# A two-layer graph attention kernel: Q of the first masked attention as a row through DRAM, behind a quarter of the graph before; carries in other PSUM banks

## The chip, the core and the metric

The kernel runs on one core of one Trainium2 chip. The time is the device time of one execution, in microseconds (us). Five runs of the kernel before have a median of 2361.38 us (2356.87 to 2363.09).

The engines go by these names: TensorE (PE; its weight loads are PEld), VectorE (DVE), ScalarE (ACT), GpSimd (POOL) and SyncE (SP), which issues transfers. Each engine takes its instructions in the order in which the program lists them.

## What is computed

Sixteen graphs of 1024 nodes with 256 features go through two layers, each on a normalised input and added back to x. One adjacency matrix serves all graphs. Cut to what matters, the reference is:

```python
def _gat(inp, adj_mask, W, a):                      # slope 0.2
    h = inp @ W
    f1, f2 = h @ a[:F_, 0], h @ a[F_:, 0]
    e = leaky_relu(f1[:, :, None] + f2[:, None, :], ALPHA)
    if adj_mask is not None:
        e = where(adj_mask[None] > 0, e, NEG_INF)
    return elu(softmax(e, axis=2) @ h)

def _L0_gnn_ref(x, adj, ...):
    out = relu(x @ mlp1_w + mlp1_b)                 # 256 -> 512
    out = elu(_gat(relu(out), None, W_fc, a_fc)) + out
    out = relu(out @ mlp2_w + mlp2_b)               # 512 -> 256
    out = elu(_gat(relu(out), adj, W_hand, a_hand)) + out
    return relu(out)

def _L1_gnn_ref(inp, adj, W, a):                    # slope 0.01, masked by adj
    return relu(softmax(e, axis=-1) @ h)

x = x + _L0_gnn_ref(relu(layernorm(x)), adj, ...)
x = x + _L1_gnn_ref(relu(layernorm(x)), adj, ...)
```

So each graph has three attentions: a dense one (no mask, 512 features), a first masked one (layer 0) and a second masked one (layer 1).

## The kernel before

**The three attentions.** The dense one isn't done as a product, except for half of graph 0. Nodes are ranked by f2 (`rank`), their rows are scattered to DRAM in that order (`scatter`), read back (`read_sorted`), and summed up from below and from above (`sum_before`, `sum_behind`). The sums go to DRAM as a fine table; the totals of each partition are summed over partitions by two small products with triangular matrices (`carry`) and written to a coarse table. Each node counts, from the sums of signs (`sign`, on ScalarE, then `count`), how many nodes lie below its threshold, and gathers its row of the fine table, then adds its row of the coarse one (`gather`, indirect transfers of GpSimd in two halves of four). `share` and `mean` turn what was gathered into the result, `merge` transposes it (hpT) for the next product.

The masked ones are products of weights with the nodes' features. The weight of node j on node i is, up to factors that cancel, the larger of Q[i] and W[j], times the mask. `vectors` makes the columns Q, W and D (tile qwd; D scales the features in `scale`). Q is needed as a row that all 128 partitions hold (`rows`). For that, `row` either broadcasts by eight transposes on TensorE into two PSUM banks and a copy on ScalarE, or, with `sent`, reads a row from DRAM into all partitions, after `send` has transposed the column, copied it and written it there. Before the change the second attention of graphs 0 to 13 goes through DRAM, and so does f2 of the dense attention (`r2`); the first attention broadcasts on TensorE. `weight` makes 128 x 256 weights on VectorE, `product` uses them for two tiles of nodes: an attention has four such quarters q, each of eight steps j. Then `finish`, `combine` and `update` (reciprocal on VectorE, exponentials on ScalarE, two adds on GpSimd for the first attention, an update of x on VectorE).

In the profile's names, tiles that end in "a" (oa, atta, hma, rowsa, pa) belong to the first masked attention, those that end in "b" (ob, attb, hmb, rowsb, pb) to the second.

**Order.** The order of every engine is written out by hand. `at(lo, hi, steps)` puts steps at planned times, in us of an ideal TensorE; all are sorted by these, and each engine takes its instructions in that order. The planned times are only an order: an engine goes on as soon as what it waits for is there. A graph b has its base at `base_of(b)` = 142 b - 28. Planned from its base: `vectors` at +1, the row at +4, the first attention's products from +11 to +39, those of the second attention of graph b-1 from +39 to +67, the norm and projection of graph b's second attention until +78, then the dense attention's merges for graph b+1, and the first projections of graph b+2. GpSimd has its own chain of dependencies in the same order; its scatters and gathers stand in it.

**Buffers.** Tiles rotate in rings by tag. `rows` has two buffers, for the dense row r2, the row of the first attention and that of the second, in the order of the program. `att` has eight. PSUM has four banks `mm` for products, two `tr` for transposes, and one pair `bc`, used for broadcasts and for `send`. The carries use `mm`.

**What the steps touch.** Lines of the kernel before: `send_row` 239 to 246, `Masked.send` and `row` 353 to 364, `weight` 373, `product` 384, Gnn0's finish 396 to 413, Gnn1's 420 to 426, `rank` 511 to 518, `scatter` 525, `sign` 548, `read_sorted` 569, `sum_before` and `sum_behind` 597 to 612, `write_table` 604, `carry` 615 to 624, `gather` 635, `share` 647, `mean` 657 and 659, `merge` 706; in the plan `dense_sums`, `gathers`, `masked_first`, `second_norm`, `masked_second` and the loop over graphs at the end.

Of the kernel before, what the change touches and what calls it, by code (L numbers as in the profile page):

```python
# [8 lines left out]
F32 = mybir.dt.float32  # L9
# [8 lines left out]
P = 128  # L18
HALF = 512
# [12 lines left out]
def fast_path(ctx: ExitStack, tc: tile.TileContext, alarm, x, adj, w1, b1, w2, b2, w_fc, a_fc,  # L32
# [21 lines left out]
    nc = tc.nc  # L54
    NB, N, F = x.shape
    H = w1.shape[1]
    NT = N // P
# [12 lines left out]
    dram = ctx.enter_context(tc.tile_pool(name="dram", bufs=1, space=bass.MemoryType.DRAM))  # L70

    def mm_psum(name):
        return psum.tile([P, HALF], F32, tag="mm", name=name, bufs=4)
# [4 lines left out]
    def bc_psum(name):  # L78
        return psum.tile([P, NH * HALF], F32, tag="bc", name=name, bufs=1)


    def load_x(b, name):
        xt = big.tile([P, NT, F], F32, tag="x", name=f"{name}_{b}", bufs=3)
        src = x[b].rearrange("(t p) f -> p t f", p=P)
        for part in ((slice(0, TH), slice(TH, NT)) if name == "xn" and b == 0 else (slice(0, NT),)):
# [17 lines left out]
                            base=0, channel_multiplier=-1)  # L103
# [75 lines left out]
    sorted_d = [nc.dram_tensor(f"sorted{k}", [N, R], F32, kind="Internal").ap() for k in range(2)]  # L179
    fine_d = [dram.tile([N + 1, 2 * K], F32, name=f"fine{k}") for k in range(2)]  # L180
    coarse_d = [dram.tile([P + 1, 2 * K], F32, name=f"coarse{k}") for k in range(2)]
    row_d = {s: [dram.tile([1, N], F32, name=f"row_{s}{k}") for k in range(2)] for s in "rb"}
    zero = work.tile([1, K], F32, tag="carry", name="zero", bufs=2)
    nc.vector.memset(zero, 0.0)
    for k in range(2):
# [33 lines left out]
    NQ = N // PAIR  # L219
    ATT = 8  # L220

    def at(lo, hi, steps):
        for i, step in enumerate(steps):
            table.append((lo + (hi - lo) * i / len(steps), len(table), step))
# [15 lines left out]
    def send_row(dst, col, name):  # L240

        ps = bc_psum(f"{name}_ps")
        nc.tensor.transpose(ps[:NT, :P], col, ident)
        line = work.tile([NT, P], F32, tag="carry", name=name, bufs=2)
        nc.scalar.copy(line, ps[:NT, :P])
        nc.sync.dma_start(dst.rearrange("o (u i) -> (o u) i", i=P), line)

    class Norm:

# [52 lines left out]
    class Masked:  # L302
# [2 lines left out]

        def __init__(self, get_hT, w_sb, slope, b, which):
            self.get_hT, self.w_sb, self.slope, self.name = get_hT, w_sb, slope, f"{which}_{b}"
            self.b = b
            self.hm = None
            self.att = {}  # L310
            self.out = {}
# [39 lines left out]
            nc.vector.tensor_scalar_max(qwd[:, 2, :], qwd[:, 2, :], D_MIN)  # L351

        def send(self):
            send_row(row_d["b"][self.b % 2], self.qwd[:, 0, :], f"line{self.name}")

        def row(self, sent=False):

            self.rows = work.tile([P, N], F32, tag="rows", name=f"rows{self.name}")
            if sent:
                nc.sync.dma_start(self.rows, row_d["b"][self.b % 2].to_broadcast([P, N]))  # L360
            else:
                rows_ps = bc_psum(f"rowsps{self.name}")
                row_broadcast(rows_ps, cols(self.qwd[:, 0, :]))
                nc.scalar.copy(self.rows, rows_ps)  # L364
# [67 lines left out]
    class Dense:  # L432
# [182 lines left out]
        def carry(self, s):  # L615
            lhsT, total = ((upto, self.all_t), (after, self.xs[0][:, 0, :]))[s]
            carry = work.tile([P, K], F32, tag="carry", name=f"carry_{self.b}_{s}", bufs=2)
            for lo, n in ((0, F + 1), (F + 1, F)):
                ps = mm_psum(f"carry_{self.b}_{s}_{lo}")
                nc.tensor.matmul(ps[:, :n], lhsT=lhsT, rhs=total[:, lo:lo + n], start=True,  # L620
                                 stop=True)
                nc.scalar.copy(carry[:, lo:lo + n], ps[:, :n])
            coarse = coarse_d[self.b % 2]
            nc.sync.dma_start(coarse[:P, K:] if s else coarse[1:P + 1, :K], carry)

# [122 lines left out]
    xs = {}  # L748
# [17 lines left out]
    def each(f, *ranges):  # L766
        out = [()]
        for r in ranges:
            out = [o + (i,) for o in out for i in r]
        return [partial(f, *o) for o in out]  # L770
# [41 lines left out]
    def dense_sums(t0, b):  # L812
        d = dense[b]
        at(t0 - 3, t0 - 3, [d.sums_begin])
        at(t0 - 22, t0 - 4, each(d.sign, range(NT)))
        for h in range(2):
            at(t0 + 6.5 + 4 * h, t0 + 6.5 + 4 * h, [partial(d.sums_weights, h)])
            at(t0 + 7.5 + 5 * h, t0 + 12.5 + 5 * h, each(d.sum_before, tiles(h)))
        at(t0 + 13, t0 + 13, [partial(d.write_table, 0, 0)])
        at(t0 + 18, t0 + 18, [partial(d.write_table, 0, 1)])  # L820
        at(t0 + 18, t0 + 32, each(d.sum_behind, range(NT - 1, -1, -1)))
        at(t0 + 25, t0 + 25, [partial(d.write_table, 1, 1)])
        at(t0 + 32, t0 + 32, [partial(d.write_table, 1, 0)])
        at(t0 + 33, t0 + 33, [d.count])
        at(t0 + 50.5, t0 + 50.5, each(d.carry, range(2)))

    def gathers(d, h, lo, hi):
        at(lo, lo + 4, each(d.gather, [h], [0], range(TH)))
        at(hi, hi + 7, each(d.gather, [h], [1], range(TH)))
# [25 lines left out]
    def weights(m, q, lo, hi):  # L855
        at(lo, hi, each(m.weight, [q], range(NT)))

    def masked_first(t0, b):
        m, n = gnn0[b], norm2[b]
        at(t0 + 1, t0 + 1, [m.vectors])  # L860
        at(t0 + 4, t0 + 4, [m.row])
        at(t0 + 4.5, t0 + 10, each(m.scale, range(NT)))
        weights(m, 0, t0 + 5.5, t0 + 10)
        at(t0 + 10, t0 + 10, [partial(load_again, b)])
        at(t0 + 4.5, t0 + 11, each(dense[b].natural, range(NT // 2)))
        at(t0 + 11, t0 + 39, each(m.product, range(NQ), range(NT)))
        for q in range(1, NQ):
            weights(m, q, t0 + 5.5 + 7 * q, t0 + 12 + 7 * q)
        for t in range(NT):
            lo = t0 + 18.2 + 7 * (t // 2) + 0.6 * (t % 2)  # L870
            at(lo, lo, [partial(m.finish, t)])
            at(lo + 1.2, lo + 1.2, [lambda t=t: m.combine(t, dense[b].o_nat)])
            at(lo + 5.2, lo + 5.2, [lambda t=t: m.update(t, xs[b])])
            at(lo + (6.2 if last(b) or b == 0 else 9), lo + (6.2 if last(b) or b == 0 else 9), [partial(n.stats, t)])
        at(t0 + 36, t0 + 36, [partial(n.root, 0)])
        lo = t0 + (46.5 if last(b) or b == 0 else 51)
        at(lo, lo, [partial(n.root, 1)])

    def last(b, n=1):
        return b >= NB - n  # L880

    def second_norm(t0, b):
        n, m = norm2[b], gnn1[b]
        if last(b):
            n.turn_at(t0 + 46.5, 0)
            n.turn_at(t0 + 49, 1, 1.6)
            lo = t0 + 50
        elif b == 0:
            n.turn_at(t0 + 47, 0)
            n.turn_at(t0 + 50.5, 1, 1.6)  # L890
            lo = t0 + 47.2
        else:
            n.turn_at(t0 + 53.3, 0)
            n.turn_at(t0 + 67.3, 1)
            lo = t0 + 71
        at(lo, lo + 7, each(m.project, range(NT)))
        at(lo + 7.5, lo + 7.5, [m.extremes])
        if last(b, 2):
            at(lo + 7.8, lo + 7.8, [m.vectors])
            at(lo + 8.2, lo + 8.2, [m.row])  # L900
            at(lo + 8.3, lo + 9.5, each(m.scale, range(NT)))
        else:
            at(lo + 11, lo + 11, [m.vectors])
            at(lo + 24, lo + 24, [m.send])
            at(lo + 40, lo + 52, each(m.scale, range(NT)))
            at(base_of(b + 1) + 22, base_of(b + 1) + 22, [partial(m.row, True)])

    def masked_second(parts, b):

# [14 lines left out]


    SHORT = 28.0

    def base_of(b):
        return b * PERIOD - SHORT * (b > 0)

# [9 lines left out]
    n = norm1[1]  # L940
# [59 lines left out]
    for b in range(NB):  # L1000
        base, after_base = base_of(b), base_of(b + 1)
        masked_first(base, b)
        second_norm(base, b)
        if last(b):
            parts = [base + 65 + 7 * q for q in range(NQ)]
        elif last(b, 2):
            parts = [base + 86, base + 94.5, base + 107.5, after_base + 39]
        else:
            parts = [after_base + 39 + 7 * q for q in range(NQ)]
        masked_second(parts, b)  # L1010
        if b + 1 < NB:
            if b:
                dense_sums(base, b + 1)
            for h in range(NH):
                if b:
                    gathers(dense[b + 1], h, base + 48 + 4 * h, base + 58 + 7 * h)
                else:
                    gathers(dense[1], h, base + 16 + 12 * h, base + 22 + 25 * h)
            dense_end(after_base - PERIOD, b + 1)
        if b + 2 < NB:  # L1020
            first_mlp(base, b + 2)
            dense_rows(after_base - PERIOD, b + 2)
            dense_begin(after_base, b + 2)
        if b + 3 < NB:
            lo = after_base - PERIOD + 86
            at(lo, lo, [partial(load_first, b + 3)])
            first_norm(after_base, b + 3)
# [465 lines left out]
```

## Time and profile before

| | |
|---|---|
| median of 5 runs | 2361.38 us |
| the profiled execution | 2360.6 us, of which 2358.9 span |
| granted TensorE clock, mean | 0.991 |
| TensorE, VectorE, ScalarE, GpSimd busy | 97%, 70%, 53%, 41% |
| products of the two masked attentions (line 384) | 455.8 + 459.7 us busy |
| a steady graph (start of one oa product to the next) | 139.9 us |

The profile is of one execution. Times in it count from the span's start. A line of the order in time has start, duration, engine, line, operation, out<-in, shape and count; in brackets the idle time before and what ended it. Neighbouring instructions of one kind are merged into one such line, and as TensorE's instructions overlap, what a group costs is read from its start to the start of the next. Each product of 32-bit floats shows as two passes, a transpose as one. The graph followed below is 5: its base lies near 859.4 us, its first oa product starts at 870.17.

### The profile page before, as it was taken

How to read it: one execution, taken by the hardware profiler on the slowest of the kernel's cores; microseconds unless marked ns; L12 is line 12 of the kernel's file. 1: busy time of each engine (PE TensorE's matmuls, PEld its weight loads, DVE VectorE, ACT ScalarE, POOL GpSimd, SP SyncE). 2: the span in 40 equal slices, each digit the busy share in tenths (PEclk: the TensorE clock that was granted, in tenths of full speed). 3: DMA queues.
4: the chain of work that ended last, by engine and by line, in shares of the span. 5: the costliest groups of instructions: out<-in, count | busy, mean ns of one | idle time of the engine just before them, and what ended most of it. 6: DMA issues, size and time to landing. Idle time of an engine off the chain costs nothing.

```text
span 2358.9 us, 31110 instructions
## 1 busy us (share of the span) xinstructions
PE 2281.7 (97%) x10053; PEld 1759.3 (75%) x10053; DVE 1639.4 (70%) x4499; ACT 1250.1 (53%) x2740; POOL 968.3 (41%) x1216
## 2 busy tenths in 40 slices
PE   8989999999999999999999999999999999999897
PEld 5666777777877777777787877777787777778666
DVE  6766685866958577685866868586686857759554
ACT  5345655646365563745646374564736556463442
POOL 1153444353534536344353634435353453535220
PEclk9999999999999999999999999999999999999898
DMA  4658256572645746265573635657264574726400
GB/s 170 169 152 214 65 156 185 154 199 89 195 107 170 188 137 188 86 182 152 168 190 116 185 98 162 176 161 197 88 199 102 167 188 142 191 80 203 109 1 29
DMA packets 148522, 348.41 MB, mean 148 GB/s; under 512 B 10776, under 2 KB 62200, under 8 KB 144256
## 3 DMA queue, kind: packets, MB, share of 16 engines
q1 hardware_dynamic: 102400, 182.36, 26.3%
q0 software_dynamic: 45952, 163.99, 25.9%
q8 instruction: 82, 1.34, 0.2%
q14 instruction: 88, 0.72, 0.1%
HBM read 220.06 MB, written 126.24 MB: 147 GB/s over the span
## 4 chain that ended last, share of the span: by engine, by line
PE 60%; DVE 30%; ACT 5%; issue 2%; POOL 2%; DMA 1%; DVEq 0%; ACTq 0%; POOLq 0%; SPq 0%
PE ob L384 12%; PE h L465 11%; PE oa L384 9%; PE m L451 8%; PE m L724 5%; DVE attb L373 5%; PE pb L322 5%; DVE atta L373 4%; DVE junk L513 4%; DVE junk L511 3%; DVE xs L612 3%; DVE x L413 2%; PE hpT L706 2%; PE pa L322 2%; DVE stats L262 2%; PE nt L282 2%
## 5 line engine op out<-in xcount | busy, mean ns | idle before, releaser
L384 PE MATMUL oa<-hma,atta 128*128 128x258 f32 x2048 | 455.8, 382 | 12.1 <-DVE atta L373 12.1
L465 PE MATMUL h<-wfc_sb,resT 128*128 128x257 f32 x2048 | 466.0, 380 | 0.0
L384 PE MATMUL ob<-hmb,attb 128*128 128x257 f32 x2048 | 459.7, 384 | 5.5 <-DVE attb L373 5.5
L384 PEld LDWEIGHTS oa<-hma,atta 128*128 128x128 f32 x2048 | 384.5, 190 | 78.5 <-DVE atta L373 23.5
L384 PEld LDWEIGHTS ob<-hmb,attb 128*128 128x128 f32 x2048 | 392.1, 192 | 62.0 <-ACT hmb L368 3.7
L465 PEld LDWEIGHTS h<-wfc_sb,resT 128*128 128x128 f32 x2048 | 378.9, 190 | 53.5 <-issue 1.0
L717 POOL TENSOR_TENSOR resT<-resT,e 128x512 f32<-128x512 f32 x128 | 163.3, 1276 | 416.6 <-DVE e L716 371.9
L373 DVE SCALAR_TENSOR_TENSOR atta<-rowsa,qwda,edge 128x256 f32<-128x256 f32 x512 | 263.6, 542 | 43.8 <-ACT rowsa L364 31.2
L373 DVE SCALAR_TENSOR_TENSOR attb<-rowsb,qwdb,edge 128x256 f32<-128x256 f32 x512 | 257.0, 531 | 30.8 <-PE ob L384 28.0
L408 POOL TENSOR_TENSOR posa<-posa,onat 128x256 f32<-128x256 f32 x120 | 106.8, 890 | 408.7 <-ACT posa L400 408.7
L451 PE MATMUL m<-hT,w_sb 128*128 128x512 f32 x512 | 236.9, 601 | 0.5 <-ACT posa L400 0.5
L399 ACT ACTIVATE ea<-oa,reca 128x256 f32<-128x256 f32 x128 | 60.8, 475 | 329.0 <-DVE reca L396 318.5
L724 PE MATMUL m<-resT,w_sb 128*128 128x512 f32 x512 | 230.8, 597 | 4.4 <-POOL resT L717 4.4
L635 POOL DMA_INDIRECT got<-coarse,k x124 | 194.6, 1570 | 39.8 <-issue 39.8
L422 ACT ACTIVATE rb<-ob,recb 128x256 f32<-128x256 f32 x128 | 57.5, 474 | 269.7 <-DVE recb L420 269.7
L708 DVE TENSOR_SCALAR e<-hpT 128x512 f32<-128x512 f32 x128 | 88.4, 691 | 150.3 <-PE hpT L706 112.4
L724 PEld LDWEIGHTS m<-resT,w_sb 128*128 128x128 f32 x512 | 94.1, 192 | 107.3 <-issue 91.6
L451 PEld LDWEIGHTS m<-hT,w_sb 128*128 128x128 f32 x512 | 92.8, 193 | 91.5 <-issue 88.8
L635 POOL DMA_INDIRECT got<-fine,k x124 | 129.6, 1045 | 61.7 <-issue 29.1
L548 ACT ACTIVATE junk<-r,fs 128x1024 int8<-128x1024 f32 x124 | 142.7, 1151 | 12.3 <-POOL fs L469 12.1
L525 POOL DMA_INDIRECT sorted<-hnat,place x128 | 131.5, 1028 | 39.5 <-issue 16.4
L709 ACT ACTIVATE e<-e 128x512 f32<-128x512 f32 x128 | 80.7, 630 | 93.3 <-DVE e L708 93.0
(183 smaller groups left out, 3495.8 us busy)
## 6 DMA issues: line engine op xcount, KB each, us to landing
xs<-sorted SPq DMA_DIRECT2D x32, 1028.0 KB
fine<-tt SPq DMA_DIRECT2D x32, 1026.0 KB
fine<-xs SPq DMA_DIRECT2D x32, 1026.0 KB
x<-in_x_dram SPq DMA_DIRECT2D x16, 1024.0 KB
out_dram<-x SPq DMA_DIRECT2D x32, 512.0 KB
xn<-in_x_dram SPq DMA_DIRECT2D x15, 1024.0 KB
coarse<-carry SPq DMA_DIRECT2D x32, 256.5 KB
r<-row_r SPq DMA_DIRECT2D x14, 512.0 KB
```

The costliest lines, as they stand in the source:

```text
L322: nc.tensor.matmul(ps[:, :2 + F], lhsT=hT[:, c, t * P:(t + 1) * P], rhs=self.w_sb[:, c, 0, :], start=(c == 0), stop=(c == FC - 1))
L373: nc.vector.scalar_tensor_tensor(a_t, self.rows[:, q * PAIR:(q + 1) * PAIR], self.qwd[:, 1, j:j + 1], edge[:, j, q * PAIR:(q + 1) * PAIR], ...
L384: nc.tensor.matmul(self.out[t][:, :F + self.ONES], lhsT=self.att[q, j][:, (t % 2) * P:(t % 2 + 1) * P], rhs=self.hm[:, j, 2:2 + F + self.O ...
L408: adder.tensor_add(pos, pos, o_nat[:, t, :])
L451: nc.tensor.matmul(ps, lhsT=w1_sb[:, kc, c * P:(c + 1) * P], rhs=hT[:, kc, h * HALF:(h + 1) * HALF], start=(kc == 0), stop=(kc == FC - 1))
L465: nc.tensor.matmul(ps[:, :F + 1], lhsT=self.resT[:, kc, t * P:(t + 1) * P], rhs=wfc_sb[:, kc, g, :], start=(kc == 0), stop=(kc == HC - 1))
L513: nc.vector.tensor_scalar(junk[:, t * P:], r2[:, t * P:], s, None, op0=OP.is_lt, op1=OP.add, accum_out=rank[:, 1, t:t + 1])
L525: made = nc.gpsimd.indirect_dma_start(out=sorted_d[self.b % 2], out_offset=bass.IndirectOffsetOnAxis(ap=self.place[:, t:t + 1], axis=0), i ...
L548: nc.scalar.activation(junk, self.r2, AF.Sign, bias=self.fs[:, 0, t:t + 1], accum_out=self.signs[:, t:t + 1])
L635: nc.gpsimd.indirect_dma_start(out=got[u // n][:, u % n, :], out_offset=None, in_=(coarse_d if coarse else fine_d)[self.b % 2][:, :], in_o ...
L717: nc.gpsimd.tensor_add(dst, dst, e)
L724: nc.tensor.matmul(ps, lhsT=w2_sb[:, kc, c * P:(c + 1) * P], rhs=self.resT[:, kc, h * HALF:(h + 1) * HALF], start=(kc == 0), stop=(kc == H ...
```

## The change

It has five parts.

1. The first attention of graphs 1 to 14 (`AHEAD`) sends Q through DRAM: `send` planned at +3.4 and the read at +6, in place of the broadcast at +4. Its products start at +18 instead of +11; its weights, finishes, statistics and roots move with them.
2. The first quarter of graph b-1's second attention (b-1 from 0 to 13) goes from +39 to +11, the other three stay at +46, +53 and +60 or move there. Its row is read at -4.5 instead of +22.
3. `carry` uses the pair `bc` instead of two `mm` banks for each; the two carries stand at +38.9 and +45.9 instead of both at +50.5. The gathers are planned 3 to 4 us sooner.
4. `send_row` issues its write from ScalarE instead of SP.
5. The signs are spread by hand from -27 to -8.2 (before: from -22, 2.25 apart, the last at -6.25). The first half of norm2 is turned at +60.3 instead of +53.3.

```diff
-    row_d = {s: [...] for s in "rb"}
+    row_d = {s: [...] for s in "rab"}
...
     def send_row(dst, col, name):
...
         nc.scalar.copy(line, ps[:NT, :P])
-        nc.sync.dma_start(dst.rearrange("o (u i) -> (o u) i", i=P), line)
+        nc.scalar.dma_start(dst.rearrange("o (u i) -> (o u) i", i=P), line)
...
         def carry(self, s):
...
-            for lo, n in ((0, F + 1), (F + 1, F)):
-                ps = mm_psum(f"carry_{self.b}_{s}_{lo}")
-                nc.tensor.matmul(ps[:, :n], lhsT=lhsT, rhs=total[:, lo:lo + n], start=True,
-                                 stop=True)
-                nc.scalar.copy(carry[:, lo:lo + n], ps[:, :n])
+            ps = bc_psum(f"carry_{self.b}_{s}")
+            parts = ((0, F + 1, 0), (F + 1, F, HALF))
+            for lo, n, bank in parts:
+                nc.tensor.matmul(ps[:, bank:bank + n], lhsT=lhsT, rhs=total[:, lo:lo + n],
+                                 start=True, stop=True)
+            for lo, n, bank in parts:
+                nc.scalar.copy(carry[:, lo:lo + n], ps[:, bank:bank + n])
...
     def dense_sums(t0, b):
-        at(t0 - 22, t0 - 4, each(d.sign, range(NT)))
+        for t, lo in enumerate((27, 25, 18.5, 16.3, 14.1, 12, 9.8, 8.2)):
+            at(t0 - lo, t0 - lo, [partial(d.sign, t)])
...
-        at(t0 + 50.5, t0 + 50.5, each(d.carry, range(2)))
+        at(t0 + 38.9, t0 + 38.9, [partial(d.carry, 0)])
+        at(t0 + 45.9, t0 + 45.9, [partial(d.carry, 1)])
...
     def masked_first(t0, b):
         at(t0 + 1, t0 + 1, [m.vectors])
-        at(t0 + 4, t0 + 4, [m.row])
-        at(t0 + 4.5, t0 + 10, each(m.scale, range(NT)))
-        weights(m, 0, t0 + 5.5, t0 + 10)
+        lo = t0 + 11
+        if b in AHEAD:
+            at(t0 + 3.4, t0 + 3.4, [m.send])
+            at(t0 + 6, t0 + 6, [partial(m.row, True)])
+            lo += 7
+        else:
+            at(t0 + 4, t0 + 4, [m.row])
+        at(t0 + 4.5, lo - 1, each(m.scale, range(NT)))
+        weights(m, 0, lo - 5.5, lo - 1)
...
-        at(t0 + 11, t0 + 39, each(m.product, range(NQ), range(NT)))
+        at(lo, lo + 28, each(m.product, range(NQ), range(NT)))
...
-        at(t0 + 36, t0 + 36, [partial(n.root, 0)])
-        lo = t0 + (46.5 if last(b) or b == 0 else 51)
+        at(lo + 25, lo + 25, [partial(n.root, 0)])
+        lo += 35.5 if last(b) or b == 0 else 38.5
         at(lo, lo, [partial(n.root, 1)])
...
     def second_norm(t0, b):
-            n.turn_at(t0 + 53.3, 0)
+            n.turn_at(t0 + 60.3, 0, 7)
             n.turn_at(t0 + 67.3, 1)
...
-            at(base_of(b + 1) + 22, base_of(b + 1) + 22, [partial(m.row, True)])
+            at(base_of(b + 1) - 4.5, base_of(b + 1) - 4.5, [partial(m.row, True)])
...
+    AHEAD = range(1, NB - 1)
...
-            parts = [after_base + 39 + 7 * q for q in range(NQ)]
+            parts = [after_base + lo for lo in (11, 46, 53, 60)]
...
-                    gathers(dense[b + 1], h, base + 48 + 4 * h, base + 58 + 7 * h)
+                    gathers(dense[b + 1], h, base + 44.5 + 3.5 * h, base + 55 + 7 * h)
```

More of the change, by code (lines that the diff above doesn't have):

```diff
@@ L181, in fast_path @@
     coarse_d = [dram.tile([P + 1, 2 * K], F32, name=f"coarse{k}") for k in range(2)]
-    row_d = {s: [dram.tile([1, N], F32, name=f"row_{s}{k}") for k in range(2)] for s in "rb"}
+    row_d = {s: [dram.tile([1, N], F32, name=f"row_{s}{k}") for k in range(2)] for s in "rab"}
     zero = work.tile([1, K], F32, tag="carry", name="zero", bufs=2)
@@ L307, in __init__ @@
             self.get_hT, self.w_sb, self.slope, self.name = get_hT, w_sb, slope, f"{which}_{b}"
-            self.b = b
+            self.b, self.which = b, which
             self.hm = None
@@ L353, in send @@
         def send(self):
-            send_row(row_d["b"][self.b % 2], self.qwd[:, 0, :], f"line{self.name}")
+            send_row(row_d[self.which][self.b % 2], self.qwd[:, 0, :], f"line{self.name}")
         def row(self, sent=False):
@@ L359, in row @@
             if sent:
-                nc.sync.dma_start(self.rows, row_d["b"][self.b % 2].to_broadcast([P, N]))
+                nc.sync.dma_start(self.rows, row_d[self.which][self.b % 2].to_broadcast([P, N]))
             else:
@@ L860, in masked_first @@
         at(t0 + 1, t0 + 1, [m.vectors])
-        at(t0 + 4, t0 + 4, [m.row])
-        at(t0 + 4.5, t0 + 10, each(m.scale, range(NT)))
-        weights(m, 0, t0 + 5.5, t0 + 10)
+        lo = t0 + 11
[7 more added lines that the diff above has]
+        weights(m, 0, lo - 5.5, lo - 1)
         at(t0 + 10, t0 + 10, [partial(load_again, b)])
         at(t0 + 4.5, t0 + 11, each(dense[b].natural, range(NT // 2)))
-        at(t0 + 11, t0 + 39, each(m.product, range(NQ), range(NT)))
+        at(lo, lo + 28, each(m.product, range(NQ), range(NT)))
         for q in range(1, NQ):
-            weights(m, q, t0 + 5.5 + 7 * q, t0 + 12 + 7 * q)
+            weights(m, q, lo - 5.5 + 7 * q, lo + 1 + 7 * q)
         for t in range(NT):
[L870 to L874, printed above, removed]
-        at(t0 + 36, t0 + 36, [partial(n.root, 0)])
-        lo = t0 + (46.5 if last(b) or b == 0 else 51)
+            end = lo + 7.2 + 7 * (t // 2) + 0.6 * (t % 2)
+            at(end, end, [partial(m.finish, t)])
+            at(end + 1.2, end + 1.2, [lambda t=t: m.combine(t, dense[b].o_nat)])
+            at(end + 5.2, end + 5.2, [lambda t=t: m.update(t, xs[b])])
+            end += 6.2 if last(b) or b == 0 else 9
+            at(end, end, [partial(n.stats, t)])
+        at(lo + 25, lo + 25, [partial(n.root, 0)])
+        lo += 35.5 if last(b) or b == 0 else 38.5
         at(lo, lo, [partial(n.root, 1)])
```

## The prediction

> **What bounds the kernel now.** I read the page's head first, then TensorE's waits over the whole run, then one steady period by stages, then the orders in time of TensorE, VectorE and GpSimd in it. The head says that TensorE is busy 97% of the span. In a steady period of 140 us it is busier still:
>
> ```profile
> PE 2281.7 (97%) x10053; PEld 1759.3 (75%) x10053; DVE 1639.4 (70%) x4499; ACT 1250.1 (53%) x2740; POOL 968.3 (41%) x1216
> ...
> 857.00:997.00 140.00, 138.76 (x615) 106.98 (x614) 99.22 (x272) 77.02 (x171) 62.50 (x78) 1.00 0.55 155
> ...
> PE oa L384 <- DVE atta L373: 12.1, 28, 0.8
> PE hpT L706 <- DVE hp L659: 6.4, 7, 1.7
> ...
> PE pa L322 <- ACT hma L324: 3.5, 14, 0.6
> ```
>
> The second line is the stretch from 857 to 997 us: its length, then busy time of TensorE, weight load, VectorE, ScalarE and GpSimd, the granted clock (1.00), the DMA share and GB/s. Only 1.2 us of 140 are idle. So a steady graph gets shorter in two ways: less TensorE work, or less of that 1.2 us; and any new wait is paid in full. The last lines are waits over the whole run (total, times, longest). The 28 waits for the weights of the first masked attention (oa) are two in each of graphs 1 to 14.
>
> Why these come is in VectorE's load by stage (same columns):
>
> ```profile
> 865.90:870.40 4.50, 4.40 (x24) 2.78 (x23) 1.67 (x4) 3.81 (x9) 0.00 (x0) 1.00 0.97 397
> 870.40:911.80 41.40, 40.47 (x185) 34.35 (x183) 40.92 (x94) 17.05 (x44) 16.74 (x20) 1.00 0.53 141
> 911.80:931.40 19.60, 19.57 (x96) 16.67 (x97) 13.12 (x40) 4.92 (x12) 15.98 (x14) 1.00 0.94 299
> ```
>
> From 870.4 to 911.8 VectorE has 40.92 of 41.40 us to do: the sums of the next graph's table, the weights, the updates. It falls behind and TensorE meets it in the last quarter. In the 4.5 us before, it waits for the sorted rows; in the 20 us after, the DMA engines are the full resource (0.94), with the gathers.
>
> **What TensorE loses of work.** Now eight broadcast transposes of Q run in each graph:
>
> ```profile
> 863.80 1.04 PE L238 MATMUL rowspsa<-ident,qwda 128*128 128x128 f32 x8
> 864.67 1.88 PE L451 MATMUL m<-hT,w_sb 128*128 128x512 f32 x4
> ...
> 911.78 1.13 PE L620 MATMUL carry<-all,upto 128*128 128x257 f32 x4
> 912.95 1.14 PE L620 MATMUL carry<-xs,after 128*128 128x257 f32 x4
> 913.92 2.76 PE L384 MATMUL ob<-hmb,attb 128*128 128x257 f32 x12
> ```
>
> They hold TensorE from 863.80 to 864.67, 0.87 us, 0.109 each (their 273 ns overlap). One transpose (send) stays, so 7 x 0.109 = 0.76 us go in each of 14 graphs (AHEAD is 1 to 14): 10.7 us. ScalarE loses the 1.01 us copy of the broadcast and gets a copy of 0.24 us (the row of line<-line_ps).
>
> The carries: from 911.78 to 913.92 they take 2.14 us for eight passes; at the rate of the products beside them (12.30 us for 56 passes, 0.220 each) they need 1.76. The other 0.38 us are waits for the evictions of the shared "mm" banks. In two free banks, 7 us apart, they go: 14 x 0.38 = 5.3 us. In graphs 0 and 1 the two carries still stand together, now with one pair of banks: the second waits for two copies, 0.81 us and a hand-over of 0.2, so +1.0 each, +2.0.
>
> **What the moved quarter does for VectorE.** Counted with the spacing of its rows (weights 0.40, sums 0.67, pairs of reciprocals 0.14, updates 0.34, statistics 0.54), VectorE has 24.3 us to do up to the last oa weights, plus 3 us of slowing beside GpSimd's adds (pairs of weights take 1.8 instead of 0.87): 27.3, from 870.4 to 897.7, where TensorE wanted them at 897.3. Afterwards 4.6 us more come ahead of them (five weights of the moved quarter, the first three fall into the gap before; its updates; four oa weights that now run in that gap; the count), and the sums begin 0.7 us sooner, with TensorE, so they end near 901.6; TensorE, with the 7 us of the moved quarter and one carry ahead, wants them at 904.4. The 12.1 us of waits go. Bounds: all 12.1, or none if VectorE slips 3 us more; I take all, the margin being 2.8 us.
>
> **The new way of Q.** The transpose is at 863.8, the copy ends near 864.4, then write and read in series. The same pair for the dense rows: write issued 832.65, read issued 833.88 (1.2 us); the 512 KB then move for some 4 us. That gives 870.0, and 872.5 when it shares the engines with the 2 MB of sorted rows (share 0.97). SP has the read behind that of the sorted rows (which waits for the scatters until 863.66) and ahead of x for the update, which goes from 864.9 to 866: needed only 20 us later. VectorE gets to the first oa weight at 874.1, as the sums and the moved quarter's weights stand before it. So the cover is 1.6 us, and 2.3 us more before TensorE needs that weight at 876.4: cost nothing; with the cover gone, each us late is a us of TensorE in 14 graphs. The row of the second attention now leaves right behind the dense row, 25 us before its use. The Trainium skill (DMA: Bandwidth & Descriptors, Anatomy of one DMA — SWDGE (gpsimd) path) puts some 2 us of fixed cost on every DMA, mostly completion, which speaks against two in series; this trace has 1.2 us for the small one; by the page Q would be 0.8 us later, still covered.
>
> An issue on ScalarE is not in this trace. Bounds: nothing, and 0.41 us (two issues of SP take 0.82); three in a graph, with ScalarE at 55%, each behind the copy it sends. I take nothing for TensorE; queued behind are evictions that have four banks.
>
> **Signs and scatters.** Two signs move to the time before the projections and the other six go up to 2 us earlier in ScalarE's order; the last now stands before the first eviction of pa, which frees the bank for TensorE's fifth pa tile. Today that sign starts at 855.11, after GpSimd has copied its column at 854.88, behind five scatters 1.5 to 1.95 us apart. With two signs (2.7 us) out of the way, the eviction that lets GpSimd begin is some 0.8 us earlier, the last sign ends near 855.5, the eviction at 855.95, and TensorE wants the bank at 855.4: 0.5 us of wait instead of 0.25 (3.5 us in all now). Bounds: -0.25 and +1.0 a graph. I take +0.25: +3.5.
>
> **Where the wait can go: the gathers.** The chain that is closest behind TensorE in a steady graph:
>
> ```profile
> 910.21 1.08 POOL L635 DMA_INDIRECT got<-fine,k  x1 [0.17 <-issue]
> ...
> 929.03 1.54 POOL L635 DMA_INDIRECT got<-coarse,k  x1 [0.30 <-issue]
> ...
> 941.18 0.16 DVE L647 TENSOR_TENSOR den<-got,qd 128x4 f32<-128x4 f32 x1 [7.73 <-DMA got<-coarse,k]
> ...
> 943.56 2.29 DVE L659 SCALAR_TENSOR_TENSOR hp<-got,den,part 128x513 f32<-128x513 f32 x3
> ...
> 945.57 0.67 PE L706 MATMUL hpT<-ident,hp 128*128 128x128 f32 x4
> ```
>
> Half 0's last coarse gather is issued at 929.03, lands at 941.2, and the last hp is there at 945.85; the fourth transpose starts at 945.90. TensorE doesn't wait, by 0.05 us. In the period before (hp until 805.11, transpose at 806.06) the slack is 0.95; over the thirteen steady graphs 0.7 on average. TensorE will be here 0.76 + 0.38 + 0.85 = 2.0 us sooner. Does the chain come sooner? The adds of the last oa quarter, which gate all gathers today, will end near 917.5, but three fine gathers go ahead of them, from about 909. Then adds, fine ones, the first coarse one, the norm's root (1.5 us) and three coarse ones follow, the last issued near 930 to 931, 1 to 2 us later than now. Landing is by the DMA engines, though (12 us after issue), and the carries' 0.51 MB (at 299 GB/s, 1.7 us) no longer lie among the gathers. Landing between 1.7 us sooner and 1.9 later; I take 0.6 sooner, on the side of the DMA's rows. The wait is 2.0 - 0.7 - 0.6 = 0.7 us, for graphs 2 to 14: 13 x 0.7 = 9.1. Bounds: no wait (2.0 - 0.7 - 1.7 is below nothing), and 2.0 - 0.7 + 1.9 = 3.2, or 41.6. The same root feeds the second half of norm2 (nt): its result is due near 927 and TensorE comes at 928.
>
> **Sum.** The profiled execution took 2360.6 us (span 2358.9 and 1.7 around it). 2360.6 - 10.7 - 5.3 - 12.1 + 2.0 + 3.5 + 9.1 = 2347.1. The median of the runs shown is 0.8 above that execution: 2348.
>
> **Rivals.** (1) *All of it comes*: the gathers keep pace with TensorE and the signs cost nothing: 2360.6 - 28.1 + 2.0 = 2334.5, 2335 for the median. For it: DMA freed of the carries; against: a slack of 0.05 to 0.95 us where 2 are taken away. (2) *Given back at hpT*: a wait of 1.9 us, 24.7: 2338.0 + 24.7 = 2362.7, no change. It takes landing 0.6 us later than now. (3) *Slower, by GpSimd's order*: the root and the adds stand among the gathers, the DMA engines can't make it up, half 0 lands 1.9 us later, and hpT waits 3.2: 2338.0 + 41.6 = 2379.6. It decides from a wait of about 2.2 us. For it: GpSimd's stream is without a gap from 909 on; against: the 12 us from issue to landing. (4) *Q isn't hidden*: the row lands 4.5 us later than I think, at 877.0, the first oa weight is there at 877.5, and TensorE waits 1.1 us: 14 x 1.1 = 15.4, 2363; the end of TensorE's waits is then only swapped for another.
>
> **Chances.** Forecast (2340 to 2356) 0.46; (1) 0.22; (2) 0.10 and (4) 0.04, both no change; (3) 0.18. What can be told from no change is about 0.2%: under 2356.7 is faster, 0.68; within 0.14; above 2366.1 slower, 0.18. The range reaches from just under rival (1) to rival (2): 2332 to 2364.
>
> **What will show it.** Right: rowspsa in two graphs only; no oa waits for atta in steady graphs; carry rows of 0.9 us; a steady period near 138.9 us. Wrong, and where: waits at hpT for hp over 2 us a graph (gathers); at pa for hma over 0.6 (signs); at nt for hn (root); at oa's first quarter for atta (Q's row late); or the first ob quarter waiting for attb.

## The result, and the profile after

The kernel after takes 2364.75 us (median of 28 runs, 2359.49 to 2373.41), the kernel before 2360.43 (50 runs, 2354.83 to 2364.08). The ratio is 1.0023, with a 95% interval of 1.0016 to 1.003: slower by 0.2%. The forecast of a gain of 0.5% was wrong, in sign too, and the time lies just above its range. The profiled execution of after took 2363.13 us (span 2361.4, clock 0.993).

First the page's head, then TensorE's waits over the whole run (total, times, longest):

```profile
PE 2262.2 (96%) x9955; PEld 1746.6 (74%) x9955; DVE 1611.6 (68%) x4499; ACT 1242.8 (53%) x2740; POOL 954.0 (40%) x1216
```

```profile
PE extpsb L238 <- DVE extb L330: 25.0, 14, 3.6
...
PE ob L384 <- DVE attb L373: 14.1, 21, 2.1
PE hpT L708 <- DVE hp L661: 6.9, 8, 1.7
PE oa L384 <- DVE atta L373: 5.2, 12, 1.6
...
PE pa L322 <- ACT hma L324: 0.8, 2, 0.4
```

The work did go: TensorE is busy for 19.5 us less (2281.7 before). But the span is 2.5 us longer, so 22.0 us of new idle time have come. The list says where: 25.0 us at extpsb and 14.1 at ob; oa gives back only 6.9 of its 12.1. In the kernel before these two rows were:

```profile
PE ob L384 <- DVE attb L373: 5.5, 3, 2.1
...
PE extpsb L238 <- DVE extb L330: 1.5, 2, 0.8
```

The stretch from 866.55 to 1006.4 is a steady period of after, from one transpose extpsa to the next. Over graphs 2 to 13 such a period takes 140.3 us on average, where before took 139.6 and the prediction had 138.9. By stages (length, busy time of TensorE, weight load, VectorE, ScalarE, GpSimd, then granted clock, DMA share, GB/s):

```profile
871.00:912.00 41.00, 40.63 (x189) 34.39 (x188) 36.59 (x83) 18.76 (x48) 9.28 (x11) 1.00 0.68 190
912.00:932.00 20.00, 18.68 (x89) 15.60 (x88) 14.01 (x44) 4.76 (x12) 17.09 (x19) 1.00 0.69 221
932.00:950.00 18.00, 17.39 (x70) 12.10 (x69) 6.33 (x20) 9.68 (x21) 10.70 (x8) 1.00 1.07 232
```

VectorE's full stage is relieved, as meant: 36.59 of 41 us, where it had 40.92 of 41.40. TensorE's idle time now lies in the two later stages, 1.32 and 0.61 us in this period.

**The wait at extpsb.** VectorE's order in time, then TensorE's:

```profile
945.80 0.17 DVE L649 TENSOR_TENSOR den<-got,qd 128x4 f32<-128x4 f32 x1 [8.36 <-DMA got<-coarse,k]
...
948.11 0.16 DVE L330 TENSOR_REDUCE extb<-hmb 128x1 f32<-128x8 f32 x1
```

```profile
948.34 0.29 PE L238 MATMUL extpsb<-ident,extb 128*128 128x128 f32 x1 [0.61 <-DVE extb L330]
```

The tile extb holds the extremes of the second attention's values hmb, and has nothing to do with the gathers. It stands behind `share` in VectorE's order, and `share` waits 8.36 us for the gathered rows. So TensorE waits for the landing of half 0 (the moment its gathered rows are there and `share` can start), through an instruction that has only its place in the queue from it. This was the meeting that the prediction priced at hpT; it comes some 2 us earlier, at extpsb.

In graphs 2 to 13, against the start of the same graph's extpsa, the fourth coarse gather has been issued (its GpSimd instruction has ended) at 68.1 us before and 70.6 after (means), and `share` starts at 78.4 before and 79.8 after. So issue is 2.5 us later, landing 1.4 us later, while TensorE comes sooner.

**The wait at ob.** GpSimd's order in time while this happens, and VectorE's:

```profile
914.61 1.11 POOL L637 DMA_INDIRECT got<-fine,k  x1 [0.20 <-issue]
916.03 0.96 POOL L637 DMA_INDIRECT got<-fine,k  x1 [0.30 <-issue]
917.30 0.94 POOL L637 DMA_INDIRECT got<-fine,k  x1 [0.30 <-ACT ea L405]
918.25 0.74 POOL L408 TENSOR_TENSOR posa<-posa,onat 128x256 f32<-128x256 f32 x1
919.07 0.72 POOL L409 TENSOR_TENSOR ea<-ea,posa 128x256 f32<-128x256 f32 x1
...
930.16 1.14 POOL L268 TENSOR_TENSOR rstd<-rstd,power 128x4 f32<-128x4 f32 x1
...
935.40 1.55 POOL L637 DMA_INDIRECT got<-coarse,k  x1 [0.30 <-issue]
```

```profile
919.83 0.42 DVE L413 SCALAR_TENSOR_TENSOR x<-ea,x 128x256 f32<-128x256 f32 x1 [2.03 <-POOL ea L409]
920.17 0.48 DVE L373 SCALAR_TENSOR_TENSOR attb<-rowsb,qwdb,edge 128x256 f32<-128x256 f32 x1
923.91 0.43 DVE L413 SCALAR_TENSOR_TENSOR x<-ea,x 128x256 f32<-128x256 f32 x1 [3.27 <-POOL ea L409]
924.26 0.48 DVE L373 SCALAR_TENSOR_TENSOR attb<-rowsb,qwdb,edge 128x256 f32<-128x256 f32 x1
```

The adds of tiles 6 and 7 now stand between the gathers. VectorE's updates wait for them (2.03 and 3.27 us), and behind each update is a weight for ob that needs nothing from it. Over the run VectorE's waits (total, times, longest) say the same; before, the first line had 93.5 and the second 3.0:

```profile
DVE den L649 <- DMA got<-coarse,k: 136.9, 25, 11.4
...
DVE x L413 <- POOL ea L409: 64.7, 29, 3.3
...
DVE atta L373 <- DMA rowsa<-row_a: 11.8, 12, 3.3
```

The last line is Q on its way. Orders of issue of the queues, and VectorE's first oa weight (in the same period):

```profile
869.43 0.27 ACTq L246 DMA_DIRECT2D row_a<-linea  x1
...
874.83 0.32 SPq L360 DMA_DIRECT2D rowsa<-row_a  x1
...
879.55 0.48 DVE L373 SCALAR_TENSOR_TENSOR atta<-rowsa,qwda,edge 128x256 f32<-128x256 f32 x1 [1.13 <-DMA rowsa<-row_a]
```

The read follows the write by 5.4 us, not by the 1.2 us that the pair of the dense row needed.

### The profile page after: what moved, and what is told of

Read it like the earlier page. It is cut to its first block, busy times and chain, and to the rows that moved or that the text cites. A ratio compares the mean times of both kernels' runs of the same rounds, so it can differ in the third digit from the quotient of the medians.

```text
span 2361.4 us, 30815 instructions
## 1 busy us (share of the span) xinstructions
PE 2262.2 (96%) x9955; PEld 1746.6 (74%) x9955; DVE 1611.6 (68%) x4499; ACT 1242.8 (53%) x2740; POOL 954.0 (40%) x1216
## 5 line engine op out<-in xcount | busy, mean ns | idle before, releaser
L384 PE MATMUL ob<-hmb,attb 128*128 128x257 f32 x2048 | 463.0, 383 | 14.2 <-DVE attb L373 14.1
L384 PEld LDWEIGHTS ob<-hmb,attb 128*128 128x128 f32 x2048 | 385.8, 191 | 78.7 <-ACT rb L422 12.6
L408 POOL TENSOR_TENSOR posa<-posa,onat 128x256 f32<-128x256 f32 x120 | 100.8, 840 | 471.6 <-ACT posa L400 471.1
L373 DVE SCALAR_TENSOR_TENSOR attb<-rowsb,qwdb,edge 128x256 f32<-128x256 f32 x512 | 237.0, 505 | 9.9 <-PE ob L384 7.3
L451 PE MATMUL m<-hT,w_sb 128*128 128x512 f32 x512 | 237.8, 603 | 0.5 <-ACT posa L400 0.5
L726 PEld LDWEIGHTS m<-resT,w_sb 128*128 128x128 f32 x512 | 93.5, 191 | 106.1 <-issue 90.4
L451 PEld LDWEIGHTS m<-hT,w_sb 128*128 128x128 f32 x512 | 93.5, 194 | 93.1 <-issue 90.7
```

The source lines that it names most:

```text
L373: nc.vector.scalar_tensor_tensor(a_t, self.rows[:, q * PAIR:(q + 1) * PAIR], self.qwd[:, 1, j:j + 1], edge[:, j, q * PAIR:(q + 1) * PAIR], ...
L384: nc.tensor.matmul(self.out[t][:, :F + self.ONES], lhsT=self.att[q, j][:, (t % 2) * P:(t % 2 + 1) * P], rhs=self.hm[:, j, 2:2 + F + self.O ...
L408: adder.tensor_add(pos, pos, o_nat[:, t, :])
L451: nc.tensor.matmul(ps, lhsT=w1_sb[:, kc, c * P:(c + 1) * P], rhs=hT[:, kc, h * HALF:(h + 1) * HALF], start=(kc == 0), stop=(kc == FC - 1))
L726: nc.tensor.matmul(ps, lhsT=w2_sb[:, kc, c * P:(c + 1) * P], rhs=self.resT[:, kc, h * HALF:(h + 1) * HALF], start=(kc == 0), stop=(kc == H ...
```

## The experiments

Each is compared with the kernel before on its own chip; times are medians.

**Is the landing of half 0 what costs?** *less_after* leaves out two of its four coarse gathers in graphs 1 to 15, and the mean of tiles 2 and 3 takes the rows of tiles 0 and 1. *less_before* does the same to the kernel before. *ext_first* keeps all gathers and puts the extremes (extb) ahead of `share`.

```diff
         def gather(self, h, coarse, u):
+            if coarse and h == 0 and u >= 2 and not self.split:
+                return
...
-        at(lo + 7.5, lo + 7.5, [m.extremes])
+        at(lo + 6.9, lo + 6.9, [m.extremes])
```

> The changed kernel without two of the four coarse gathers of half 0 in graphs 1 to 15 (mean then uses the rows of tiles 0 and 1 for tiles 2 and 3, so those tiles' dense attention is left wrong). Theory G (the gathered rows of half 0 land too late for TensorE, and that eats the gain): landing comes some 5 us sooner, the 25.0 us of waits of extpsb for extb vanish, and the time falls from 2364.8 to some 2340. Rival O (VectorE's other lateness, Q's late row and updates behind GpSimd's adds, is what costs): waits move elsewhere and the time stays above 2355.

> The kernel before, with the same two gathers left out (tiles 2 and 3 of half 0 get the rows of tiles 0 and 1). Theory G: TensorE did not wait for the gathers there, so nothing: 2360 within 3 us. If the gathers bounded the kernel before too, it falls by more than 10 us.

> The changed kernel with extremes of the second attention ahead of share in VectorE's order, so that extps waits for the gathers no longer. Theory G: the wait only moves 1.7 us on, from extpsb to hpT, and the time stays within 4 us of 2364.8. Rival (only VectorE's order costs, hpT itself has room): the 25 us go, and the time falls to 2340 to 2345.

*less_after*: 2335.16 us, 0.9882 (0.9867 to 0.9897). *less_before*: 2357.78, 0.9989 (0.998 to 0.9998). *ext_first*: 2363.79, 1.0015 (1.0006 to 1.0025). Two gathers less bring some 30 us where TensorE has been made faster, and 3 where it hasn't: a gain of the expected size is there, and half 0 keeps it back. It isn't the expected sum term by term: in the profiled execution of *less_after* the wait at extpsb is the 1.5 us of before, while ob still waits 16.6 us. The edit also takes bytes from the DMA engines, so it doesn't yet say why half 0 is late. With the extremes ahead of `share` the wait at extpsb is again the 1.5 us of before, but hpT, where TensorE needs the gathered rows themselves, has taken it over: 12.8 us more of waits (6.9 us in 8 waits in after), and hpT's rows busy for 84.5 us instead of 77.8:

```profile
PE hpT L708 <- DVE hp L661: 19.7, 39, 1.7
```

So the order of extb and `share` is only where the lateness shows.

**What makes half 0 late: GpSimd's order or the DMA engines?** *dve_adds* puts the adds of tiles 6 and 7 of the first attention, in graphs 1 to 14, on VectorE. *adds_first* leaves them on GpSimd and puts all gathers behind them, as they stood before. *dve_adds_before* is the first edit on the kernel before.

```diff
-            adder = nc.vector if self.beside_gathers else nc.gpsimd
+            adder = nc.vector if self.beside_gathers or (self.b in AHEAD and t >= 6) else nc.gpsimd
...
-                    gathers(dense[b + 1], h, base + 44.5 + 3.5 * h, base + 55 + 7 * h)
+                    gathers(dense[b + 1], h, base + 48.1 + 3.5 * h, base + 55.2 + 7 * h)
```

> The changed kernel with the two adds of tiles 6 and 7 of the first attention on VectorE instead of GpSimd, in graphs 1 to 14. Theory P (GpSimd's stream, with those adds and the root among the gathers, makes half 0 late): four adds of 0.73 us go out of the stream, the last coarse gather of half 0 is issued some 3 us sooner, it lands 2 to 3 us sooner, extpsb's 25 us of waits go to under 5, and the updates no longer wait for GpSimd, so ob's waits fall from 14 to 6: some 2335 to 2340. Theory D (the DMA engines are full, so issue does not matter): landing stays, only ob's waits go: some 2356.

> The changed kernel with the gathers planned from +48.1, behind all adds of the first attention. Theory P: GpSimd idles some 1 us for the adds' operands and the stream ends that much later; extpsb waits 35 to 40 us in all, ob's waits fall by 8: 2366 to 2372. If the updates behind the adds were what costs, not the landing: some 2356.

> The kernel before with the same two adds on VectorE. TensorE waits there for VectorE's weights and not for the gathers, and VectorE has no room until 911.8: no gain, 2360 to 2366. If the gathers bound the kernel before as well, it gets faster.

*dve_adds*: 2329.12 us, 0.9879 (0.9858 to 0.99), faster than both kernels and some 6 us below the expected 2335. GpSimd's stretch of the same gathers, in this run:

```profile
901.10 1.08 POOL L637 DMA_INDIRECT got<-fine,k  x1 [0.20 <-issue]
902.48 0.96 POOL L637 DMA_INDIRECT got<-fine,k  x1 [0.30 <-issue]
903.75 1.18 POOL L637 DMA_INDIRECT got<-fine,k  x1 [0.30 <-issue]
905.23 0.96 POOL L637 DMA_INDIRECT got<-fine,k  x1 [0.30 <-issue]
...
914.04 1.07 POOL L268 TENSOR_TENSOR rstd<-rstd,power 128x4 f32<-128x4 f32 x1
...
919.14 1.55 POOL L637 DMA_INDIRECT got<-coarse,k  x1 [0.30 <-issue]
```

From the first fine gather to the start of the fourth coarse one it is 18.0 us, against 20.8 in after (914.61 to 935.40); over graphs 2 to 13 the means are 18.1 and 20.8, and 18.2 in before. The first fine gather starts at the same place in all three, 47.7 to 48.3 us behind extpsa, so the later issue of after is these adds. Issue is 3.3 us sooner on average (67.3 against 70.6), `share` 3.7 us sooner (76.0 against 79.8). The DMA engines move the same bytes, so it was not they that kept half 0 late. The weights for ob no longer stand behind an add on another engine. TensorE's waits (extpsb is back at the 1.5 us of before; ob is not, 9.6 where 6 were expected):

```profile
PE ob L384 <- DVE attb L373: 9.6, 16, 2.1
...
PE oa L384 <- DVE atta L373: 1.8, 6, 0.4
...
PE extpsb L238 <- DVE extb L330: 1.5, 2, 0.8
```

*adds_first*: 2411.55 us, 1.0225 (1.0209 to 1.024): the sign was right and the size far off. The waits:

```profile
PE nt L282 <- DVE hn L272: 36.9, 22, 9.8
PE extpsb L238 <- DVE extb L330: 36.7, 15, 3.4
```

The wait at ob is the old 5.5 us, so the adds among the gathers did cause that one. Half 0 comes later still (`share` at 81.3), and now the root is late as well (nt waits 21.2 us more than in after). In the profiled executions (2403.36 and 2363.13 us) these waits and the ones that shrink make 20.8 us; the other 20.1 are TensorE's busy time, 2282.3 instead of 2262.2 for the same instructions. Of it 13.6 lie in the products m behind extpsb (251.4 instead of 237.8) and 5.6 in nt, at a mean granted clock of 0.981 instead of 0.993; the last section has the reason.

*dve_adds_before*: 2396.52 us, 1.0163 (1.0148 to 1.0179), where no gain was expected and a loss of 36 us came. VectorE's order at the tiles 6 and 7:

```profile
915.09 0.42 DVE L408 TENSOR_TENSOR posa<-posa,onat 128x256 f32<-128x256 f32 x1 [0.90 <-ACT posa L400]
916.66 0.43 DVE L409 TENSOR_TENSOR ea<-ea,posa 128x256 f32<-128x256 f32 x1 [1.15 <-ACT ea L406]
917.00 0.51 DVE L373 SCALAR_TENSOR_TENSOR attb<-rowsb,qwdb,edge 128x256 f32<-128x256 f32 x1
```

Directly behind the last oa quarter VectorE has no lead: it waits for ScalarE's eviction and exponential, 2.05 us in this graph, with the weights for ob behind, and ob's waits go from 5.5 to 33.1 us. The same edit gains 1.5% of the kernel after (2364.75 to 2329.12) and costs 1.6% of the kernel before.

**Does Q's row cost?** *sp_send* takes part 4 back: the row is written from SP's queue.

```diff
-        nc.scalar.dma_start(dst.rearrange("o (u i) -> (o u) i", i=P), line)
+        nc.sync.dma_start(dst.rearrange("o (u i) -> (o u) i", i=P), line)
```

> The changed kernel with the three row writes issued from SP again. Now the read of Q's row is issued 5.4 us after its write, where the quiet write took 1.2, as 2 MB of sorted rows are under way. If that is the shared DMA engines, the queue makes no difference or SP's is worse (its write stands behind the sorted rows in one queue): 2364.8 to 2370. If the second queue itself costs: faster by 5 or more.

2390.28 us, 1.0129 (1.0105 to 1.0153), some 26 us more than after and 20 above what was expected. SP's issues and TensorE's wait:

```profile
875.98 0.28 SPq L246 DMA_DIRECT2D row_a<-linea  x1
883.20 0.32 SPq L360 DMA_DIRECT2D rowsa<-row_a  x1
```

```profile
PE oa L384 <- DVE atta L373: 17.7, 28, 2.2
```

Behind the sorted rows in SP's queue the 4 KB take 7.2 us, and oa waits 12.5 us more than in after. TensorE's busy time grows by another 17.1 (2279.3), again for the same instructions and at a lower granted clock (0.988). The prediction had taken part 4 as free; it was worth these 26 us.

**The smaller parts, alone.** *carry_alone* and *sign_alone* are the kernel before with part 3 without the move of the gathers, and with the signs of part 5.

```diff
-        at(t0 + 50.5, t0 + 50.5, each(d.carry, range(2)))
+        at(t0 + 38.9, t0 + 38.9, [partial(d.carry, 0)])
+        at(t0 + 45.9, t0 + 45.9, [partial(d.carry, 1)])
...
-        at(t0 - 22, t0 - 4, each(d.sign, range(NT)))
+        for t, lo in enumerate((27, 25, 18.5, 16.3, 14.1, 12, 9.8, 8.2)):
+            at(t0 - lo, t0 - lo, [partial(d.sign, t)])
```

> The kernel before with the carries alone changed: in the bc banks, at +38.9 and +45.9, gathers where they were. By the prediction's sum 14 x 0.38 = 5.3 us less and 2.0 more in graphs 0 and 1: some 2357. Theory G adds that 0.38 us a graph fits in the slack of 0.7 at hpT, so it should come; if it does not, the slack is smaller than read.

> The kernel before with the signs' order alone changed. The prediction had pa's waits for hma grow by 3.5 us; in the changed kernel they fell from 3.5 to 0.8. If the order of the signs did that, they fall here too, and the time by 2 to 3 us, 2357.5, near what can be told; if not, pa's waits stay at 3.5 or grow to 7.

*carry_alone*: 2361.88 us, 1.0004 (0.9995 to 1.0013): nothing, where 3 to 4 us were expected. The carries' products did get shorter, 38.7 us instead of 41.4 in the run, but the next meeting took it, the turn of norm2, where the kernel before has 15.8 us in 8 waits:

```profile
PE nt L282 <- DVE hn L272: 18.5, 17, 9.9
```

*sign_alone*: 2356.8 us, 0.998 (0.997 to 0.9989), a gain of 3.6 us, and the waits at pa for hma fall from 3.5 us to 0.9.

**Do they matter beside the adds?** *dve_carry_back* is dve_adds with `carry` and its time as before the change; *dve_adds_ext* is dve_adds with the extremes ahead of `share`.

> dve_adds with the carries back in the mm banks, both at +50.5. If the prediction's 0.38 us a graph is real and only hidden where something later in the graph is the bound (carry_alone gave nothing, as the turn of norm2 then waited), it must show here, where TensorE has no long wait: 14 x 0.38 = 5.3 us, less 2.0 at the start: 2329.1 + 3.3, some 2332; more if the 0.5 MB among the gathers makes half 0 late again. If the carries' banks never mattered: 2329 within 2.

> dve_adds with extremes ahead of share. Half 0 now lands some 3 us before TensorE comes, so no wait is left to move: 2329 within 3 us. If the order behind share still cost, it gets faster by more than 4.

*dve_carry_back*: 2363.99 us, 1.0011 (0.9998 to 1.0024), about 32 more than expected. TensorE's waits, and GpSimd's:

```profile
PE carry L620 <- ACT carry L622: 18.3, 15, 1.3
...
PE carry L620 <- ACT posa L400: 7.8, 14, 0.6
```

```profile
POOL got L635 <- DMA coarse<-carry: 30.7, 14, 3.0
```

At the old time the banks "mm" still hold the last oa quarter, which the change has moved there, and the coarse table comes 2 to 3 us late for the first coarse gather. A part that alone is worth nothing is worth some 30 us in the new order.

*dve_adds_ext*: 2334.6 us, 0.989 (0.9876 to 0.9905), no gain over dve_adds (0.9858 to 0.99). That is 5.5 us above dve_adds and outside the expected 3, but the two ran on different chips and their intervals overlap.

## Why the prediction was wrong

The sum by its own terms, for the profiled executions; measured values are differences of the rows and waits of the two traces:

| term | predicted us | measured us |
|---|---|---|
| seven transposes of Q | -10.7 | -10.8 (rowspsa 16.7 to 2.1, linea_ps 3.8 new) |
| carries | -5.3 + 2.0 | -3.1 (products -2.7, pauses 2.3 to 1.9) |
| oa waits for atta | -12.1 | -6.9 |
| pa waits for hma | +3.5 | -2.7 |
| half 0 of the gathers | +9.1 | +24.0 (extpsb +23.5, hpT +0.5) |
| ob waits for attb | 0 | +8.6 |
| not in the sum | 0 | -6.6 |
| span | -13.5 | +2.5 |

The last line but one is what is left; 6.0 of it is busy time of TensorE outside the rows and carries. The carries are part of it: read from start to start, as the prediction did, they take 1.74 us instead of 2.14 in each of graphs 2 to 15, 5.6 us, and 1.1 more in graphs 0 and 1, together -4.5 instead of -3.1. The transposes on and nt are the largest other groups (busy for 2.9 and 2.6 us less); why stays open. The execution of the table has the highest clock of after's 30 (0.993; the median is 0.9885), so it is not the typical one.

**Right:** the work that TensorE loses (10.8 us of transposes for 10.7, 0.40 us a graph of carries for 0.38), and that the closest chain behind it, GpSimd's gathers, decides. Rival (1), "all of it comes", at 2335, is near what *less_after* measured when the chain was lightened, 2335.16; that it is the same number is luck, as ob waited there and *dve_adds* went below it. GpSimd's issue was right too: "the last issued near 930 to 931" is 930.82 in after, once the 4.58 us are taken off by which this graph's extpsa starts later.

**The step that failed:** "Landing is by the DMA engines, though … I take 0.6 sooner, on the side of the DMA's rows." The 12 us from issue to landing were read as a queue in full DMA engines that would swallow a later issue. With issue 2.5 us later, landing is 1.4 later: the engines made up 1.1, where the step let them make up 1.6 to 2.6 (issue 1 to 2 later, landing 0.6 sooner). *dve_adds* settles it: the same bytes, issued 3.3 us sooner, are there 3.7 us sooner. The wait is then 2.0 us on average in twelve steady graphs (0.6 to 3.6), in place of 0.7 in thirteen. That is rival (3)'s mechanism, "by GpSimd's order", at 24.0 us instead of 41.6. That the time ends near rival (2)'s 2362.7 is chance: it takes the waits at ob, which no rival had.

**What was not foreseen:** the prediction counted GpSimd's adds as something in the way of the gathers, but not the gathers as something in the way of the adds. Those are the +8.6 at ob: VectorE's updates wait for adds behind gathers, and weights stand behind the updates. Its list of signs did name "the first ob quarter waiting for attb", but its sum put this term at nothing without a reason.

**Sizes off:** Q's row (the write taken at 1.2 us from a quiet stage, measured 5.4 beside 2 MB of sorted rows), and the waits at oa, of which 6.9 of 12.1 us went. How much of that shortfall is Q's was not separated: in *dve_adds* the row takes as long (4.7 to 5.6 us in all graphs but one) and oa waits only 1.8, so most of it goes with the adds among the gathers. And the signs: their new order was priced as a loss of 3.5 us and was a gain, 2.7 us of waits in after and 3.6 us of time alone.

## What to carry to other kernels

Work taken from the engine that sets the time is worth the smallest slack of the chains that meet it later, and no more: look for the meeting, and for what has only its place in a queue from that chain (extb behind `share`). Where instructions of two kinds share an in-order engine, price both directions, what each makes the other wait for. Try a helper edit in the schedule it is meant for: adds on VectorE were worth -1.5% after the change and +1.6% before it, and the carries nothing alone and 30 us within it.

## What the runs showed of the hardware

**The clock after a short pause.** In *adds_first* TensorE waits 3.37 us at extpsb; its order in time, and the same stretch by windows (columns as above):

```profile
958.09 0.44 PE L238 MATMUL extpsb<-ident,extb 128*128 128x128 f32 x1 [3.37 <-DVE extb L330]
958.33 3.15 PE L451 MATMUL m<-hT,w_sb 128*128 128x512 f32 x4
```

```profile
957.00:959.00 2.00, 0.91 (x2) 0.61 (x3) 1.88 (x5) 1.71 (x4) 0.00 (x0) 0.62 1.06 222
959.00:961.00 2.00, 2.00 (x4) 0.78 (x3) 1.85 (x7) 1.87 (x5) 0.00 (x0) 0.53 1.07 227
961.00:965.00 4.00, 4.00 (x23) 3.33 (x22) 1.90 (x5) 2.77 (x7) 0.00 (x0) 1.00 1.08 228
```

The granted clock falls to 0.62 and 0.53 in these two windows, and the four passes take 3.15 us; in after, behind short waits, four such passes take 1.88. So a long wait is paid once as a wait and once more, by some 1.5 us, in slow passes behind it. It isn't a fixed length: in *adds_first* eleven of the twelve waits at extpsb that took 2.24 us or more were followed by slow passes (3.15 to 3.62 us), one of 3.0 us wasn't; in after those up to 2.78 weren't, the one of 3.60 was. The traces' record of the granted clock shows why: apart from the one at the run's end, slow stretches last 3.41 us or a multiple of it and start on a grid of 3.41 us that the kernel's waits don't move. Of the 32 waits of more than 1.5 us at extpsb in *adds_first*, *sp_send* and after, all 17 with 1.96 us or more within one cell of that grid were followed by a slow stretch, and none of the 15 with at most 1.94; the 3.0 us wait was split into 1.07 and 1.94. The Trainium skill (TensorE: Matmul & The Clock Gate, Part 1: The HAM clock gate) puts the fall behind an idle window of some 3.4 us that runs free of the kernel; the grid agrees, but the fall is seen here behind pauses clearly shorter than that. After's wide spread goes with this clock: of its 30 executions the six at 0.985 to 0.987 took 2364.77 to 2373.41 us, the six at 0.990 to 0.993 took 2359.49 to 2365.16. That the waits at extpsb are what lowers it there is not shown, as only the trace of one of the latter is kept.

**A small write beside large transfers.** A row of 4 KB was written and confirmed (from the issue of the write to the issue of the read that waits for it) in 1.2 us in a quiet stage (DMA share 0.01 from 832 to 834 us of before), in 5.4 from ScalarE's queue beside the 2 MB of sorted rows (share 0.94 from 869 to 875 us of after), and in 7.2 from SP's queue, in which those rows were ahead of it. The Trainium skill (DMA: Bandwidth & Descriptors, Issuing engines are not separate DMA queues) says that issuing from several engines saves only the time of initiating; the 1.8 us between the last two, and the 26 us of *sp_send*, are more than that (issuing the write takes 0.28 us in *sp_send*'s row). The skill's fixed cost of some 2 us, which the prediction set beside its own 1.2 and which its section gives for GpSimd's path, lies between the quiet and the loaded measurement: the small write took less in a quiet stage and more than twice as much beside the large transfers.
